# Reordering the steps in which an image leaves: stores between the scans, decays before squares, power between multiplications, adding DMAs thinned out, z fetched earlier

## The chip, the cores and the metric

The kernel runs on one core of a Trainium2 chip. The metric is the device time of one launch in microseconds (us). The five engines are called by their names and, in profile lines, by short forms: TensorE (PE for matmuls, PEld for weight loads), VectorE (DVE), ScalarE (ACT), GpSimd (POOL) and SyncE (SP), which here only issues DMAs. L891 in a profile line is line 891 of the kernel.

## The reference

The input is eight images of 128 x 128 positions with 128 channels. A first layer (an attention with a linear cost, a layer norm and a residual) gives x. A second layer, a selective scan in four directions, uses it. Cut to what matters, with `z` and `u` made from x by a projection and a small convolution, over L = 16384 positions and 256 channels:

```python
delta = softplus(dt_weight @ dt + dt_bias)          # per direction
dA    = exp(delta * A)
xc    = dA * xc + delta * u * B                     # a scan along L
y_dir = xc * C + u * D
...
y   = y0 + y1 + y2 + y3                             # the four directions, turned back
yz  = y * silu(z)
yn  = (yz - mean(yz)) / sqrt(var(yz) + 1e-5) * gamma + beta      # over the 256 channels
out = yn @ Wout
```

## The kernel before, in words

There are three stages: `layer0`, `layer1_front` and `layer1_scan`. The first two keep in DRAM what the third needs: `ubs` (u times B), `xps` (the rows for delta and for C, as three bfloat16 parts), `zs` (silu of z) and `gs` (the sums of u times D). The change touches the third stage alone, `layer1_scan`, which in the trace begins at about 5010 us of 10095.

The third stage walks 512 units. An output image has four slots, one for each direction, and a slot has NCH = 16 chunks of CH = 1024 positions: 8 x 4 x 16 units. All 256 channels lie as two halves c of 128 partitions. The sum y of one image stays in SBUF whole (`y`, 128 x 2 x 16384 float32). The first slot of an image (`place` 0) writes y, the other three add to it.

For every unit n, `step(n)` issues the following, and `in_order` makes each engine keep exactly the order in which its instructions are issued. So the text of `step` is the schedule: an engine never passes an instruction that waits.

- `load_rows` and `load` bring the rows (three buffers) and the unit `ubt` (1 MB, four buffers, three units ahead) through SyncE's queue. At the start of a slot, `load_rows` also loads small weights (L813, L814).
- `delta(n + 1, c)` multiplies the rows into PSUM (L873). `soften` is a softplus on ScalarE (L877), `decay` an exponential in place in PSUM (L881). The two functions need different tables, so each pair has a table load ahead of it.
- `weigh` multiplies the unit by the softened delta on GpSimd (L884).
- `scan` runs the recurrence on VectorE (L891 forwards, L893 backwards), once for each half c; `state` (L901) keeps the last column.
- `spread` makes C on all partitions with a matmul (L907). `emit` multiplies by C one step later on VectorE (L919 in the first slot; L924, L931 and L935 in the others), `gather` (L943, VectorE) and `add` (L950, GpSimd) add to y.

When the four slots of an image are through, its y leaves in 16 pieces of 1024 positions, one in each of the first 16 steps of the next image's first slot. `leaving` maps a step to the image and piece; `now`, `last` and `soon` are the pieces of this step, the step before and the next one. I call these steps the leaving steps. For a piece:

- `fetch` loads z (two tiles of 512 KB, a ring of five), `gate` multiplies y by z, the first half on GpSimd and the second on VectorE (L970), one step ahead.
- `square` (L973, ScalarE) writes the squares, `moments` (L983, TensorE) sums both over the channels, `keep` (L989, ScalarE) and `to_tokens` (L995, TensorE) turn the sums, `variance` (L999 to L1003, VectorE) makes the variance, and `deviation` (L1006, GpSimd) raises it to the power -0.5.
- `project` (L1013, TensorE) multiplies by Wout into the PSUM bank that the scan of the second half has just left. `store` (L1019, VectorE, and the DMA L1023) scales and writes out, one step later.

Two resources tie these together. PSUM has three pairs of banks, each of 1024 columns, (`px`) which delta, decay, scan, project and store pass on to each other in a ring. And the moments, the turned moments and the second spread share one bank (tag "pt"), so the second spread waits until `variance` has copied the moments (L999).

`add_d` (L844) is a DMA from GpSimd's queue which adds 1 MB of `gs` to a piece of y in SBUF. `summed` gives the step in which each piece has it.

Of the kernel before, what the change touches and what calls it, by code (L numbers as in the profile page):

```python
# [21 lines left out]
NC2 = 2  # L22
R = 8
K = 4
# [7 lines left out]
NCH = L // CH  # L32
# [655 lines left out]
def layer1_scan(ctx: ExitStack, tc, ubs, xps, zs, gs, dtw, dtb, a_log, gamma, beta, w_out, out):  # L688
# [15 lines left out]
    nc = tc.nc  # L704
# [128 lines left out]
    units = []  # L833
# [5 lines left out]
    ubt, sp, da, st = {}, {}, {}, {}  # L839
# [6 lines left out]
    def load_rows(n):  # L846
        sl, i = units[n]
        m = sl.at(i)
        if i == 0:
            sl.weights()  # L850
        rw = rws[n % 3]
        md = NCH - 1 - m if sl.dt_turned_back else m
        src = xps[sl.dt_image, sl.dt_order].rearrange("j r l -> (j r) l")
        for j in range(3):
            nc.sync.dma_start(rw[3 * NR * j : 3 * NR * j + 3 * NR, :], src[:, md * CH : md * CH + CH])
        nc.sync.dma_start(rw[96:99, :], xps[sl.b, sl.order, :, R + 1, m * CH : m * CH + CH])

    def load(n):
        sl, i = units[n]
        m = sl.at(i)  # L860
        ubt[n] = wp.tile([P, NC2, CH], F32, name="ubt", tag="ub", bufs=4)
        nc.sync.dma_start(ubt[n], ubs[sl.b, sl.order].rearrange("c p l -> p c l")[:, :, m * CH : m * CH + CH])

    def delta(n, c):
        sl, i = units[n]
        rw = rws[n % 3]
        da[n, c] = p = px.tile([P, CH], F32, name="px")
        for hf in range(2):
            if sl.dt_turned_back:
                src = rw[:, (1 - hf) * 512 : (1 - hf) * 512 + 512][:, ::-1]  # L870
            else:
                src = rw[:, hf * 512 : hf * 512 + 512]
            nc.tensor.matmul(p[:, hf * 512 : hf * 512 + 512], sl.dw[:, c * P : c * P + P], src, start=True, stop=True)  # L873

    def soften(n, c):
        sp[n, c] = t = wp.tile([P, CH], F32, name="sp", tag="sp", bufs=3)
        nc.scalar.activation(t, da[n, c], AF.Softplus)  # L877

    def decay(n, c):
        sl, i = units[n]  # L880
        nc.scalar.activation(da[n, c], sp[n, c], AF.Exp, scale=sa[:, sl.s, c : c + 1])  # L881

    def weigh(n, c):
        nc.gpsimd.tensor_tensor(ubt[n][:, c, :], ubt[n][:, c, :], sp.pop((n, c)), ALU.mult)  # L884

    def scan(n, c):
        sl, i = units[n]
        x, e = da[n, c], ubt[n][:, c, :]
        start = 0.0 if i == 0 else st[n - 1][:, c : c + 1]
        if sl.back:  # L890
            nc.vector.tensor_tensor_scan(e[:, ::-1], x[:, ::-1], e[:, ::-1], start, ALU.mult, ALU.add)  # L891
        else:
            nc.vector.tensor_tensor_scan(e, x, e, start, ALU.mult, ALU.add)  # L893
# [11 lines left out]
    def spread(n, hf, tag):  # L905
        cps[n, hf] = p = pe.tile([P, 1, GN], F32, name="pc", tag=tag)
        nc.tensor.matmul(p[:, 0, :], csel, rws[n % 3][:, hf * 512 : hf * 512 + 512], start=True, stop=True)  # L907

    def emit(n, hf):

        sl, i = units[n]
        h = ubt[n][:, :, hf * 512 : hf * 512 + 512]
        c = cps.pop((n, hf)).to_broadcast([P, NC2, GN])
        if sl.place == 0:
            v = sl.y_at(i, hf)
            split = "p c (a b) -> p c a b"
            nc.vector.tensor_tensor(v, h.rearrange(split, b=H), c.rearrange(split, b=H), ALU.mult)  # L919
            if hf == 1:  # L920
                ubt.pop(n)
            return
        if hf == 1:
            nc.vector.tensor_tensor(h, h, c, ALU.mult)  # L924
            return
        p = da.pop((n, 1))
        if sl.y_turned:
            ts[n] = p.rearrange("p (c b a) -> p c b a", c=NC2, a=GW)
            t = p.rearrange("p (c b a) -> p c a b", c=NC2, a=GW)
            split = "p c (a b) -> p c a b"  # L930
            nc.vector.tensor_tensor(t, h.rearrange(split, b=H), c.rearrange(split, b=H), ALU.mult)  # L931
        else:
            t = p.rearrange("p (c q) -> p c q", c=NC2)
            ts[n] = t.rearrange("p c (a b) -> p c a b", b=H)
            nc.vector.tensor_tensor(t, h, c, ALU.mult)  # L935
# [19 lines left out]
    def piece(m, hf):  # L955
        return y[:, :, (2 * m + hf) * GN : (2 * m + hf + 1) * GN]

    def mirrored(o, m, hf):
        p = 2 * m + hf
        return 2 * NCH - 1 - p if o % 2 == 1 else p  # L960

    def fetch(o, m):
        for hf in range(2):
            zt[m, hf] = z = wp.tile([P, NC2, GN], F32, name="z", bufs=5)
            p = mirrored(o, m, hf)
            nc.sync.dma_start(z, zs[o].rearrange("c p l -> p c l")[:, :, p * GN : p * GN + GN])

    def gate(o, m, hf, eng):
        z, ym = zt[m, hf], piece(m, hf)
        eng.tensor_tensor(z, ym[:, :, ::-1] if o % 2 == 1 else ym, z, ALU.mult)  # L970

    def square(m, hf):
        nc.scalar.activation(piece(m, hf), zt[m, hf], AF.Square)  # L973

    def moments(m):

        pm = pe.tile([P, GN], F32, name="pm", tag="pt")
        for c in range(NC2):
            for j in range(2):
                for hf in range(2):  # L980
                    at = 32 * (2 * j + hf)
                    v = piece(m, hf) if j else zt[m, hf]
                    nc.tensor.matmul(pm[at : at + 32, :], mean, v[:, c, :], start=(c == 0), stop=(c == NC2 - 1))  # L983
        pts[m, "rows"] = pm

    def keep(m):
        pm = pts[m, "rows"]
        pts[m, "rows"] = sr = wp.tile([P, GN], F32, name="sr", bufs=1)
        nc.scalar.copy(sr, pm)  # L989

    def to_tokens(m):
        sr = pts.pop((m, "rows"))
        pts[m] = p = pe.tile([P, GW, NC2, 2], F32, name="pq", tag="pt")
        for w in range(GW):
            nc.tensor.matmul(p[:, w], sr[:, w * H : w * H + H], sel, start=True, stop=True)  # L995
# [9 lines left out]
    def deviation(m):  # L1005
        nc.gpsimd.tensor_tensor(rst[m], rst[m], half, ALU.pow)  # L1006
# [17 lines left out]

    leaving, summed = {}, {}
    for o in range(B):
        for j in range(NCH):
            m = NCH - 1 - j if o % 2 == 1 else j  # L1030
            leaving[(o + 1) * K * NCH + j] = o, m
            summed[((o + 1) * K - 1) * NCH + j + 3] = o, m
    N = len(units)

    def step(n):
        live = 0 <= n < N
        then = n + 1 < N
        before = 1 <= n <= N
        now, last, soon, fresh = (leaving.get(n + i) for i in (0, -1, 1, 2))
        if before:  # L1040
            emit(n - 1, 0)
            if units[n - 1][0].place:
                gather(n - 1)
            emit(n - 1, 1)
        if n + 2 < N:
            load_rows(n + 2)
        if now:
            for hf in range(2):
                square(now[1], hf)
            moments(now[1])  # L1050
        if last:
            for hf in range(2):
                store(*last, hf)
        if live:
            for c in range(NC2):
                decay(n, c)
            for c in range(NC2):
                weigh(n, c)
        if soon:
            gate(*soon, 0, nc.gpsimd)  # L1060
        if then:
            delta(n + 1, 0)
        if now:
            keep(now[1])
            to_tokens(now[1])
        if live:
            scan(n, 0)
            da.pop((n, 0))
        if then:
            delta(n + 1, 1)  # L1070
        if live:
            scan(n, 1)
            state(n)
        if now:
            variance(now[1])
        if then:
            for c in range(NC2):
                soften(n + 1, c)
        if soon:
            gate(*soon, 1, nc.vector)  # L1080
        if live:
            spread(n, 0, "pc")
            spread(n, 1, "pt")
        if now:
            p = da.pop((n, 1)) if live else px.tile([P, CH], F32, name="px")
            for hf in range(2):
                project(now[1], hf, p[:, hf * 512 : hf * 512 + 512])
        elif live and units[n][0].place == 0:
            da.pop((n, 1))
        if before and units[n - 1][0].place:  # L1090
            add(n - 1)
        if now:
            deviation(now[1])
        if n in summed:
            add_d(*summed[n])
        if n + 3 < N:
            load(n + 3)
        if fresh:
            fetch(*fresh)

    with in_order(tc):
        for n in range(2):
# [73 lines left out]
```

## Time and profile before

| | us |
|---|---|
| median of three runs | 10100.93 |
| lowest and highest | 10088.13, 10116.6 |
| span of the profiled run | 10095.5 |

| engine | busy us | share of the span |
|---|---|---|
| VectorE | 8259.1 | 82% |
| GpSimd | 7140.6 | 71% |
| ScalarE | 7135.9 | 71% |
| TensorE, matmuls | 6506.4 | 64% |
| TensorE, weight loads | 3272.1 | 32% |

The shares are means over three stages with different limits, so they don't say what limits the third. The costs of one instruction that matter here, as the groups of the page and the trace give them:

| line | engine, operation | mean ns |
|---|---|---|
| L884 | GpSimd, weigh | 2482 |
| L970 | GpSimd, gate | 2387 |
| L1006 | GpSimd, power | 2349 |
| L950 | GpSimd, add (half a piece) | 1616 |
| L891, L893 | VectorE, scan | 2334 |
| L970 | VectorE, gate | 1523 |
| L1019 | VectorE, store (eight in a step) | 342 |
| L877, L881 | ScalarE, soften, decay | 1024, 1109 |
| L973 | ScalarE, square | 1054 |

A mean can hide two kinds of the same instruction. The gate on VectorE has a median of 1226 ns and a longest of 6372 ns; the power on GpSimd takes 1.66 us in one step of the trace and 2.48 in another.

### The profile page before, as it was taken

How to read it: one execution, taken by the hardware profiler on the slowest of the kernel's cores; microseconds unless marked ns; L12 is line 12 of the kernel's file. 1: busy time of each engine (PE TensorE's matmuls, PEld its weight loads, DVE VectorE, ACT ScalarE, POOL GpSimd, SP SyncE). 2: the span in 40 equal slices, each digit the busy share in tenths (PEclk: the TensorE clock that was granted, in tenths of full speed). 3: DMA queues.
4: the chain of work that ended last, by engine and by line, in shares of the span. 5: the costliest groups of instructions: out<-in, count | busy, mean ns of one | idle time of the engine just before them, and what ended most of it. 6: DMA issues, size and time to landing. Idle time of an engine off the chain costs nothing.

```text
span 10095.5 us, 89685 instructions
## 1 busy us (share of the span) xinstructions
PE 6506.4 (64%) x24190; PEld 3272.1 (32%) x24352; DVE 8259.1 (82%) x9060; ACT 7135.9 (71%) x8098; POOL 7140.6 (71%) x4224
## 2 busy tenths in 40 slices
PE   8889999988678667876433635436354363553735
PEld 5555555553223222322100403204032040320503
DVE  6556776566889888988799898998989989899797
ACT  5556655556788777777687686776867768677685
POOL 3444555455475667876589798897978979789697
PEclk9999999999889888988755756557565575655757
DMA  2333223324674778877657658576485764857748
GB/s 89 128 127 127 84 97 116 128 101 158 215 269 167 244 244 256 244 238 245 238 158 201 203 154 243 161 200 205 150 243 162 202 204 153 236 165 196 209 150 224
DMA packets 1034805, 1851.19 MB, mean 183 GB/s; under 512 B 274852, under 2 KB 500772, under 8 KB 1026112
## 3 DMA queue, kind: packets, MB, share of 16 engines
q1 hardware_dynamic: 999488, 1711.23, 52.0%
q0 software_dynamic: 34816, 134.23, 6.7%
q8 instruction: 199, 3.26, 0.1%
q14 instruction: 302, 2.47, 0.1%
HBM read 1153.03 MB, written 692.12 MB: 183 GB/s over the span
## 4 chain that ended last, share of the span: by engine, by line
DVE 30%; POOL 10%; issue 4%; DMA 4%; PE 1%; ACT 1%; SPq 0%; POOLq 0%; DVEq 0%; another core or an unknown queue 0%; ACTq 0%
DVE ubt L891 9%; DVE ubt L893 8%; POOL ubt L884 5%; DVE y L943 3%; DVE ubt L924 3%; DVE px L931 3%; POOL rstd L1006 2%; DVE r L1019 2%; POOL y L950 2%; DMA z<-zs 2%; DMA rows<-xps 1%; DMA ubt<-ubs 1%; POOL y L844 1%; POOL z L970 1%; DVE state L901 1%
## 5 line engine op out<-in xcount | busy, mean ns | idle before, releaser
L884 POOL TENSOR_TENSOR ubt<-ubt,sp 128x1024 f32<-128x1024 f32 x1024 | 2455.0, 2482 | 107.4 <-ACT sp L877 91.4
L873 PE MATMUL px<-rows,dtw 128*128 128x512 bf16 x1886 | 913.4, 578 | 2274.0 <-DVE y L943 882.6
L504 POOL TENSOR_TENSOR tap<-tap 128x1024 f32<-128x1024 f32 x512 | 1206.7, 2367 | 717.4 <-ACT tap L502 618.0
L512 DVE SCALAR_TENSOR_TENSOR acc<-xb,cw,acc 128x1024 f32<-128x1024 f32 x1024 | 1320.5, 1290 | 51.0
L494 PE MATMUL acc<-xi,wt 128*128 128x512 f32 x2048 | 982.9, 624 | 569.9 <-ACT ures L519 569.5
L877 ACT ACTIVATE sp<-px 128x1024 f32<-128x1024 f32 x1024 | 1041.2, 1024 | 398.1 <-PE px L873 307.9
L950 POOL TENSOR_TENSOR y<-y,ubt 128x512 f32<-128x512 f32 x768 | 1187.9, 1616 | 117.3 <-DVE ubt L924 113.0
L873 PEld LDWEIGHTS <-dtw 128*128 128x128 bf16 x2048 | 180.2, 115 | 3061.7 <-issue 906.5
L891 DVE TENSOR_TENSOR_SCAN ubt<-px,state,ubt 128x1024 f32<-128x1024 f32 x480 | 1100.6, 2334 | 10.9 <-POOL ubt L884 7.6
L881 ACT ACTIVATE px<-sp,sa 128x1024 f32<-128x1024 f32 x1024 | 1103.2, 1109 | 6.1
L893 DVE TENSOR_TENSOR_SCAN ubt<-px,state,ubt 128x1024 f32<-128x1024 f32 x480 | 1100.5, 2334 | 8.0 <-POOL ubt L884 4.3
L502 ACT ACTIVATE tap<-xb,cw 128x1024 f32<-128x1024 f32 x768 | 833.4, 1139 | 154.2 <-DVE acc L510 91.2
L877 ACT ACT_TABLE_LOAD x512 | 656.9, 1283 | 314.9 <-PE px L873 288.8
L1013 PEld LDWEIGHTS px<-wg,z 128*128 128x128 f32 x4096 | 722.9, 274 | 212.8 <-issue 203.3
L494 PEld LDWEIGHTS acc<-xi,wt 128*128 128x128 f32 x2048 | 395.9, 199 | 1138.0 <-ACT ures L519 675.1
L274 POOL TENSOR_TENSOR q<-q,qs 128x512 f32<-128x512 f32 x256 | 271.4, 1060 | 680.8 <-DVE qs L273 680.8
L1013 PE MATMUL px<-wg,z 128*128 128x128 f32 x4096 | 715.8, 356 | 0.0
L881 ACT ACT_TABLE_LOAD x512 | 656.9, 1283 | 9.1
L907 PE MATMUL pc<-rows,csel 128*128 128x512 bf16 x1024 | 532.1, 601 | 179.7 <-DVE mv L999 170.2
L1006 POOL TENSOR_TENSOR rstd<-rstd,half 128x8 f32<-128x8 f32 x128 | 300.7, 2349 | 422.9 <-DVE rstd L1003 420.7
L467 PE MATMUL pxb<-xi,wi 128*128 128x512 f32 x1024 | 498.5, 609 | 29.0 <-ACT xh L607 24.7
L1019 DVE SCALAR_TENSOR_TENSOR r<-px,rstd,bw 128x128 f32<-128x128 f32 x1024 | 276.5, 342 | 293.4 <-issue 229.6
(159 smaller groups left out, 15373.1 us busy)
## 6 DMA issues: line engine op xcount, KB each, us to landing
ubt<-ubs SPq DMA_DIRECT2D x512, 1024.0 KB
zs<-z SPq DMA_DIRECT2D x512, 256.0 KB
ubs<-ures SPq DMA_DIRECT2D x256, 512.0 KB
ubs<-turned SPq DMA_DIRECT2D x256, 512.0 KB
y<-gs POOLq DMA_DIRECT2D x128, 1024.0 KB, 13.1
z<-zs SPq DMA_DIRECT2D x256, 512.0 KB
rows<-xps SPq DMA_DIRECT2D x1536, 60.0 KB
xi<-x SPq DMA_DIRECT2D x120, 576.0 KB
```

Source lines behind the costliest of these rows:

```text
L494: nc.tensor.matmul(acc[:, s, :], wt[:, j, c, :], x, start=(j == 0), stop=(j == len(ON_PE) - 1))
L502: nc.scalar.activation(t, at(n, c, *d), AF.Copy, scale=cw[:, c, tap(*d) : tap(*d) + 1])
L504: nc.gpsimd.tensor_tensor(sums[n, c], sums[n, c], t, ALU.add)
L512: nc.vector.scalar_tensor_tensor(acc, at(n, c, *d), cw[:, c, tap(*d) : tap(*d) + 1], acc, ALU.mult, ALU.add)
L873: nc.tensor.matmul(p[:, hf * 512 : hf * 512 + 512], sl.dw[:, c * P : c * P + P], src, start=True, stop=True)
L877: nc.scalar.activation(t, da[n, c], AF.Softplus)
L881: nc.scalar.activation(da[n, c], sp[n, c], AF.Exp, scale=sa[:, sl.s, c : c + 1])
L884: nc.gpsimd.tensor_tensor(ubt[n][:, c, :], ubt[n][:, c, :], sp.pop((n, c)), ALU.mult)
L891: nc.vector.tensor_tensor_scan(e[:, ::-1], x[:, ::-1], e[:, ::-1], start, ALU.mult, ALU.add)
L893: nc.vector.tensor_tensor_scan(e, x, e, start, ALU.mult, ALU.add)
L950: nc.gpsimd.tensor_tensor(v[:, c], v[:, c], h[:, c], ALU.add)
L1013: nc.tensor.matmul(po[:, w, :], z[:, c, w * H : w * H + H], wg[:, c, :], start=(c == 0), stop=(c == NC2 - 1))
```

## The change

The order within `step` is written anew, and the dictionaries that place the DMAs are changed:

- Stores of the last piece stand between the two scans, where they stood ahead of both.
- Decays (and the first weigh) stand ahead of the squares and moments.
- The power of the last piece stands in the next step between the two weighs, where it stood at the end of its own step.
- Both halves of delta stand after the stores, and `to_tokens` after them and after the softens; before, `to_tokens` stood between the two halves.
- Both gates stand after the spreads; the one on GpSimd stood after the weighs, with nothing of GpSimd in between, so its place in GpSimd's own order is the same but for the power.
- The adding DMAs come every 1.5 steps instead of every step: piece j in step 3 + (3j + 1) // 2 of the image's last slot, so that seven of the sixteen fall into leaving steps.
- z for the first two pieces is fetched four steps ahead of leaving, where it was two; for the others it stays two.
- In the first slot of an image the unit load is issued early in the step.

What it is for: to let the stores wait less for the projection, to have the first scan fed earlier, to take load off the DMA while an image finishes, and to have z in SBUF when the first pieces leave.

The core of the diff:

```diff
-    leaving, summed = {}, {}
+    leaving, summed, fetched = {}, {}, {}
     for o in range(B):
+        n = (o + 1) * K * NCH
         for j in range(NCH):
-            m = NCH - 1 - j if o % 2 == 1 else j
-            leaving[(o + 1) * K * NCH + j] = o, m
-            summed[((o + 1) * K - 1) * NCH + j + 3] = o, m
+            e = o, NCH - 1 - j if o % 2 == 1 else j
+            leaving[n + j] = e
+            fetched[n + j - 2 if j > 1 else n + j - 4] = e
+            summed[n - NCH + 3 + (3 * j + 1) // 2] = e
...
         if n + 2 < N:
             load_rows(n + 2)
+        if first and n + 3 < N:
+            load(n + 3)
+        if live:
+            for c in range(NC2):
+                decay(n, c)
+            weigh(n, 0)
+        if last:
+            deviation(last[1])
+        if live:
+            weigh(n, 1)
         if now:
             for hf in range(2):
                 square(now[1], hf)
             moments(now[1])
+        if live:
+            scan(n, 0)
+            da.pop((n, 0))
         if last:
             for hf in range(2):
                 store(*last, hf)
-        if live:
+        if then:
             for c in range(NC2):
-                decay(n, c)
-            for c in range(NC2):
-                weigh(n, c)
-        if soon:
-            gate(*soon, 0, nc.gpsimd)
-        if then:
-            delta(n + 1, 0)
+                delta(n + 1, c)
         if now:
             keep(now[1])
+        if then:
+            for c in range(NC2):
+                soften(n + 1, c)
+        if now:
             to_tokens(now[1])
-        if live:
-            scan(n, 0)
-            da.pop((n, 0))
-        if then:
-            delta(n + 1, 1)
         if live:
             scan(n, 1)
             state(n)
         if now:
             variance(now[1])
-        if then:
-            for c in range(NC2):
-                soften(n + 1, c)
-        if soon:
-            gate(*soon, 1, nc.vector)
         if live:
             spread(n, 0, "pc")
             spread(n, 1, "pt")
+        if soon:
+            gate(*soon, 0, nc.gpsimd)
+            gate(*soon, 1, nc.vector)
...
-        if now:
-            deviation(now[1])
+        if n + 3 < N and not first:
+            load(n + 3)
         if n in summed:
             add_d(*summed[n])
-        if n + 3 < N:
-            load(n + 3)
-        if fresh:
-            fetch(*fresh)
+        if n in fetched:
+            fetch(*fetched[n])
```

More of the change, by code (lines that the diff above doesn't have):

```diff
@@ L1038, in step @@
         before = 1 <= n <= N
-        now, last, soon, fresh = (leaving.get(n + i) for i in (0, -1, 1, 2))
+        now, last, soon = (leaving.get(n + i) for i in (0, -1, 1))
+        first = before and units[n - 1][0].place == 0
         if before:
             emit(n - 1, 0)
-            if units[n - 1][0].place:
+            if not first:
                 gather(n - 1)
@@ L1089, in step @@
             da.pop((n, 1))
-        if before and units[n - 1][0].place:
+        if before and not first:
             add(n - 1)
-        if now:
-            deviation(now[1])
+        if n + 3 < N and not first:
+            load(n + 3)
         if n in summed:
             add_d(*summed[n])
-        if n + 3 < N:
-            load(n + 3)
-        if fresh:
-            fetch(*fresh)
+        if n in fetched:
+            fetch(*fetched[n])
     with in_order(tc):
```

## The prediction

> **What bounds the kernel now.** I first read the page's busy times and slices for the stage that the change touches, then the windows of single steps in that stage, then its waits, then the timeline of one step.
>
> ```profile
> PE 6506.4 (64%) x24190; PEld 3272.1 (32%) x24352; DVE 8259.1 (82%) x9060; ACT 7135.9 (71%) x8098; POOL 7140.6 (71%) x4224
> DVE  6556776566889888988799898998989989899797
> ```
>
> No engine is full over the span, and the last half of the slices (the scan stage, from about 5010 us) has VectorE at 8 to 9 tenths with dips. The dips come once per image. A window from first scan to first scan of neighbouring steps gives the length of a step:
>
> ```profile
> 8047.20:8066.87 19.67, 4.99 (x18) 1.74 (x22) 9.74 (x8) 9.47 (x9) 10.41 (x7) 0.50 0.68 188
> 8066.87:8086.56 19.69, 11.42 (x70) 6.19 (x64) 11.53 (x19) 9.53 (x10) 13.28 (x8) 0.76 0.74 206
> 8086.56:8105.06 18.50, 11.08 (x57) 8.45 (x60) 14.89 (x19) 9.00 (x9) 12.15 (x6) 0.68 1.05 288
> 8179.00:8192.60 13.60, 10.51 (x63) 8.19 (x64) 10.82 (x19) 9.38 (x10) 9.48 (x5) 0.75 0.67 209
> 8292.82:8424.13 131.31, 46.89 (x96) 9.24 (x97) 130.14 (x97) 108.32 (x96) 122.01 (x62) 0.50 0.50 154
> 7990.40:7998.60 8.20, 2.96 (x7) 0.57 (x6) 8.13 (x7) 6.77 (x6) 8.20 (x6) 0.50 1.05 275
> ```
>
> (Columns: length, busy PE, PEld, DVE, ACT, POOL, clock, DMA share, GB/s.) Sixteen plain steps take 131.31, 8.2 each, and VectorE fills 130.14 of it: nothing to gain there. The sixteen steps in which an image leaves take 13.6 once settled with VectorE busy only 10.82, and 18.5 to 19.7 at the start, with VectorE half idle. The stretch from the last step ahead of leaving to the end of leaving (17 steps, by the first scans in VectorE's timeline) is 246.7, 245.6, 247.7, 246.7, 245.6, 249.4 and 247.2 us for the seven images that leave while the next scans: mean 247.0. The eighth leaves alone, in the last 143.5 us.
>
> What makes 13.6 of 10.82 is in the waits of a settled stretch and in the timeline:
>
> ```profile
> DVE r L1019 <- issue: 24.2, 9, 2.7
> PE pc L907 <- DVE mv L999: 13.7, 8, 1.7
> 8175.48 6.12 PE L1013 MATMUL px<-wg,z 128*128 128x128 f32 x32
> 8181.70 2.16 DVE L1019 SCALAR_TENSOR_TENSOR r<-px,rstd,bw 128x128 f32<-128x128 f32 x8 [2.65 <-issue]
> 8183.77 4.58 DVE L891 TENSOR_TENSOR_SCAN ubt<-px,state,ubt 128x1024 f32<-128x1024 f32 x2
> 8188.47 0.17 DVE L999 COPY mv<-pq 128x16 f32<-128x16 f32 x1
> 8189.06 6.16 PE L1013 MATMUL px<-wg,z 128*128 128x128 f32 x32
> ```
>
> The project ends at 8175.48 + 6.12 = 8181.60 and the stores begin at 8181.70, so "issue" hides the wait for it (in the tail the waits name it: PE px L1013). The loop is project 6.16, stores 2.1, scans 4.6, then the copy of the moments that frees the bank in front of the second spread, and project again: 13.6. The start of leaving is another matter:
>
> ```profile
> 8034.58 12.77 SPq L813 DMA_DIRECT2D dtw<-wparts  x9
> 8051.40 0.89 SPq L966 DMA_DIRECT2D z<-zs  x2
> 8057.53 2.34 POOL L970 TENSOR_TENSOR z<-y,z 128x1024 f32<-128x1024 f32 x1 [9.26 <-DMA z<-zs]
> 8059.29 1.66 DVE L970 TENSOR_TENSOR z<-y,z 128x1024 f32<-128x1024 f32 x1 [7.51 <-DMA z<-zs]
> ```
>
> The adding DMA of every step fills the DMA (share 1.05 at 275 GB/s in the window at 7990), small weight loads take 12.77 us to issue, z is asked for only behind them and arrives 6 to 8 us later.
>
> **What the Trainium skill says.** "SBUF — State Buffer", section "SBUF: two separate sides": VectorE with two SBUF inputs and a GpSimd operation that reads SBUF exclude each other for a whole instruction. The trace agrees:
>
> ```profile
> 8094.61 5.10 POOL L884 TENSOR_TENSOR ubt<-ubt,sp 128x1024 f32<-128x1024 f32 x2
> 8095.56 5.24 DVE L970 TENSOR_TENSOR z<-y,z 128x1024 f32<-128x1024 f32 x1 [3.47 <-DMA z<-zs]
> 9982.61 2.35 POOL L970 TENSOR_TENSOR z<-y,z 128x1024 f32<-128x1024 f32 x1 [3.49 <-DMA z<-zs]
> 9982.70 2.30 DVE L1003 TENSOR_SCALAR rstd<-rstd 128x8 f32<-128x8 f32 x1
> ```
>
> A 1.22 us gate took 5.24 beside two weighs, and a 0.17 us operation 2.30 beside a GpSimd gate; the scans and stores, with one operand in PSUM, do not show it. "TensorE: Matmul & The Clock Gate", section "What's actually happening": the clock is half unless TensorE was busy of late. Here the project takes 6.16 at a mean clock of 0.75 and 3.82 in the tail at 0.94.
>
> **The change part by part.** I lay out one settled leaving step from the start of emit (0), with the measured durations.
>
> Stores between the scans: emit ends at 2.3, scan 0 at 4.6, stores at 6.75, scan 1 at 9.0, copy of moments 9.1 to 9.25, three variance operations to 9.85, the VectorE gate to 10.95. The project of this step starts at about 9.7 and ends 3.82 to 6.16 later, at 13.5 to 15.9, which is 2.6 to 5.0 of the next step; its stores are due at 4.6. The wait of 2.65 is gone or nearly so. VectorE alone then gives 10.95.
>
> New waits of that order: delta of the next unit needs the PSUM bank that the stores read, so it starts at 6.8 and, now both halves together, holds back to_tokens on TensorE: delta 1.2 to 2.0, to_tokens 1.0 to 1.8, so the moments come at 9.0 to 10.6 where VectorE wants them at 9.1. The loop through TensorE is stores 2.2 + delta + to_tokens + copy 0.3 + spread 0.4 to 0.6 + project = 9.0 with all fast, 11.3 with only the project slow, 13.1 with all slow.
>
> Decays ahead of squares: ScalarE has softens to about 9.6, table 1.28 and decays 2.15 to 13.0, squares 2.1, then moments on TensorE (1.2 to 2.4 after the last square), keep 0.6, table 1.28: ready for the softens again at about 7.4 of the step, before delta is there (7.5). So ScalarE hides behind delta, and decay is never waited for by scan 0. I cost this at nothing.
>
> Power between the weighs: GpSimd has weigh 2.35, power 1.66, weigh 2.35, gate 2.36 = 8.7, with an adding DMA (1.2) 9.9, under 10.95. Queued behind the power is weigh 1, awaited by scan 1 at 6.75; it ends at about 4. Hidden. But the first weigh of the next unit is released by its soften at about 8.6 and runs to 10.95. It reads SBUF while VectorE comes to its variance operations at 9.3. By the lock they wait until 10.95, end at 11.5, and the gate at 12.7: +1.6. Power itself needs the variance, so GpSimd then stands and VectorE gets through. If the weigh starts after 9.8 the gate goes first, and the step is 11.0. I take 12.6, since soften follows the stores by fixed times.
>
> Adding DMAs every 1.5 steps: one costs (1.05 - 0.50) x 8.2 = 4.5 us of DMA time. In the last slot the load falls from 8.6 to 4.1 + 3.0 = 7.1 per 8.2 us; the small delays there (3, 0, 2, 2, 0, 3, 2 us beyond 15 x 8.2) should half vanish: -6 in all. Seven of the sixteen now fall into leaving: 0.67 x 13.6 = 9.1, + 3.0 = 12.1 of DMA time at a reachable share of 1.05 = 11.6 us a step, still below 12.6.
>
> z sooner: the first two pairs are asked for two steps earlier, four of five buffers. Each pair (1 MB) takes about 3.4 us of DMA, worked out from a plain step: 0.50 x 8.2 = 4.1 us for the unit's 1 MB and 0.19 MB of rows, which briefly overfills two steps and leaves 3 us of backlog that the unit loads, two steps ahead, absorb. Step by step: the last step before leaving becomes emit 3.66 + scans 4.6 + state + gate 1.2 and a lock wait, 11.5; the first leaving step about 12 (no stores yet, but GpSimd still has the two adds, 3.5). The extra load order for the first slot only moves a load ahead of the stores in SyncE's queue: nothing.
>
> Sum: 11.5 + 12 + 15 x 12.6 = 212.5 against 247.0, -34.5, times 7 = -241.5; -6 from the slot before. The tail's 7.35 us loop runs through TensorE and has no scans: 0; adds during it may cost some us, earlier z gives as much back. 10101 - 247.5, about 9853.
>
> **The rivals.**
> - No lock wait: the weigh starts late or the variance slips through. For it: in the settled stretch of before they never meet. Against: the release times above. 15 x 11.1: 190 per image, -57 x 7 - 6: 9696.
> - A TensorE loop or late z takes the wait's place: half clock in most of the chain, 13.1, or z behind adding DMAs, 13.5. For it: clock 0.75 now, and the second z half still waits for a project. Against: denser work raises the clock. 15 x 13.3: 223, -24 x 7 - 6: 9927.
> - Slower: the gate is held back not by one weigh but by power and the second weigh as well, as at 8095.56 (+4.0). 10.95 + 1.6 + 4.0 = 16.5 a step: 271, +24 x 7: 10269. Against: such back-to-back running followed an adding DMA there, and power needs VectorE first.
>
> **How the numbers follow.** Chances: forecast 50, no lock wait 18, TensorE or z 20, slower 12 in 100. The range 9695 to 9970 holds the first three but for the edges. Faster 0.86 (the first three, less a remainder), same 0.03, slower 0.11.
>
> **What would show it.** Right: "DVE r L1019 <- issue" gone, settled steps near 12.6 with variance or gate operations of 1.5 to 2.5 us beside L884, no idle of 7 us for z at the start. Wrong: settled steps of 11.0 (lock), of 13 or more with VectorE waiting for the moments (TensorE) or z, or gates of 4 to 6 us in most steps.

## The result, and the profile after

| | before | changed |
|---|---|---|
| median, us | 10098.44 (10088.13 to 10116.6) | 9866.85 (9859.01 to 9874.97) |
| ratio, 95% interval | | 0.9769 [0.9752, 0.9786] |
| span of the profiled run, us | 10095.5 | 9860.3 |

The change made the kernel 2.3% faster, 232 us by the medians; 9853 was predicted. I read the same views in the same order. First the page's busy times and VectorE's slices:

```profile
PE 6392.8 (65%) x24352; PEld 3116.9 (32%) x24352; DVE 8364.1 (85%) x9060; ACT 7121.7 (72%) x8098; POOL 7143.2 (72%) x4224
DVE  6556775566898888888889999999999999999996
```

The dips in the last half of the slices, one for each image, are gone. But VectorE is busy for 8364.1 us where it was 8259.1, with as many instructions (9060): some of its instructions have become longer. The windows of steps (length, busy PE, PEld, DVE, ACT, POOL, clock, DMA share, GB/s), for the image that was shown of before. The first two are the last two steps ahead of leaving, the next two are single leaving steps, each from first scan to first scan; the last holds some five leaving steps:

```profile
7891.96:7903.30 11.34, 2.72 (x6) 0.72 (x6) 8.33 (x8) 5.71 (x6) 6.96 (x5) 0.50 1.06 301
7903.30:7917.58 14.28, 3.47 (x8) 0.94 (x10) 9.49 (x7) 6.66 (x7) 11.52 (x7) 0.50 0.62 163
7929.67:7940.89 11.22, 9.71 (x64) 5.76 (x62) 10.80 (x19) 9.17 (x10) 10.27 (x6) 1.00 1.02 298
7952.13:7967.16 15.03, 9.68 (x62) 5.59 (x58) 14.89 (x18) 12.03 (x12) 11.52 (x6) 0.98 1.02 313
8050.00:8113.24 63.24, 47.42 (x328) 36.43 (x328) 62.46 (x97) 49.49 (x48) 48.76 (x22) 0.92 0.76 227
```

In the leaving steps VectorE is now full (14.89 of 15.03, 62.46 of 63.24), yet the step of 15.03 holds 4.09 us more of VectorE than that of 11.22, with one instruction fewer. In these lines TensorE's clock is 0.92 to 1.00 where it was 0.75. Ahead of leaving (the first two lines) VectorE still idles by 3.0 and 4.8 us. The DMA is full in the first of these steps (1.06), but not in the second (0.62).

VectorE's waits over the whole last stage (what waited and for what: us in total, times, longest), before:

```profile
DVE r L1019 <- issue: 229.6, 83, 4.0
DVE z L970 <- DMA z<-zs: 118.1, 22, 8.9
...
DVE px L935 <- PE pc L907: 3.5, 4, 1.2
```

and after:

```profile
DVE mv L999 <- PE pq L995: 47.8, 19, 6.5
DVE px L935 <- PE pc L907: 31.8, 15, 3.9
DVE r L1019 <- DMA out<-r: 20.1, 10, 4.3
...
DVE z L970 <- DMA z<-zs: 7.1, 3, 3.4
...
DVE r L1019 <- issue: 0.4, 1, 0.4
```

The stores' wait for the project (229.6) is gone from the leaving steps, and the gate's wait for z (118.1) is down to 7.1, in the tail. L935 has grown, one emit that waits for a spread in the last steps ahead of leaving. L999, VectorE's copy of the moments, has grown from 26.0 (before, all of it in the tail) to 47.8: 25.4 in the first leaving steps of the seven images, 22.4 in the tail. What fills VectorE in their place is in no list of waits, as it lies inside the instructions. VectorE's timeline in one settled step (start, us, instruction):

```profile
7973.91 0.17 DVE L999 COPY mv<-pq 128x16 f32<-128x16 f32 x1
7974.11 2.02 DVE L1001 TENSOR_TENSOR rstd<-mv 128x8 f32<-128x8 f32 x1
7976.17 0.17 DVE L1002 TENSOR_TENSOR rstd<-mv,rstd 128x8 f32<-128x8 f32 x1
7976.37 0.17 DVE L1003 TENSOR_SCALAR rstd<-rstd 128x8 f32<-128x8 f32 x1
7976.45 1.23 DVE L970 TENSOR_TENSOR z<-y,z 128x1024 f32<-128x1024 f32 x1
...
7987.02 2.34 DVE L1002 TENSOR_TENSOR rstd<-mv,rstd 128x8 f32<-128x8 f32 x1
```

and GpSimd's at the same time:

```profile
7973.77 2.34 POOL L884 TENSOR_TENSOR ubt<-ubt,sp 128x1024 f32<-128x1024 f32 x1 [1.48 <-issue]
7976.62 2.58 POOL L1006 TENSOR_TENSOR rstd<-rstd,half 128x8 f32<-128x8 f32 x1 [0.51 <-DVE rstd L1003]
...
7986.99 2.34 POOL L884 TENSOR_TENSOR ubt<-ubt,sp 128x1024 f32<-128x1024 f32 x1 [0.77 <-issue]
```

The weigh begins at 7973.77 and ends at 7976.11; an operation of 128 x 8 on VectorE which takes 0.17 us elsewhere ends just behind it, at 7976.13. In the next step the same happens to L1002 (7986.99 to 7989.33, and 7989.36). GpSimd's next instruction, the power, needs VectorE's L1003, so nothing of GpSimd runs when the gate (1.23) begins, and the gate is not held. In the step of 15.03 two operations are held: L1002 for 2.25 us beside GpSimd's gate, which z had made late, and L1003 for 2.27 us beside the weigh behind it. L1003 has one input tensor only, so the hold isn't confined to operations with two inputs in SBUF, as the prediction's words have it; its own L1003 line (2.30) shows this too.

To see where the time went I added up the last stage by slots, from first scan to first scan in VectorE's timeline, over all images. Slot 0 is the one in which the image before leaves, slot 3 the one that gets the adding DMAs, the tail is from the last scan to the end:

| us | slot 0 | slot 1 | slot 2 | slot 3 | tail | sum |
|---|---|---|---|---|---|---|
| before | 1705 | 1050 | 1051 | 1134 | 143.5 | 5084 |
| changed | 1497 | 1065 | 1051 | 1099 | 154.8 | 4867 |
| changed, a second time | 1501 | 1065 | 1051 | 1100 | 155.6 | 4873 |

(Some 14 us between slots 0 and 1 are no cost: with the stores behind the first scan, that scan, which is the mark, comes 2 us earlier in a leaving step, and there are seven such boundaries.) The sum falls by 217 and 211. The rest of the difference of the two profiled spans, 18 us, lies ahead of the stage: the first scan is at 4993 in this profile and at 5012 before. Whether it belongs to the change is asked below.

### The profile page after: what moved, and what is told of

Same layout as the page of the kernel before. It is cut to its first block, busy times and chain, and to the rows that moved or that the text cites. A ratio compares the mean times of both kernels' runs of the same rounds, so it can differ in the third digit from the quotient of the medians.

```text
span 9860.3 us, 90189 instructions
## 1 busy us (share of the span) xinstructions
PE 6392.8 (65%) x24352; PEld 3116.9 (32%) x24352; DVE 8364.1 (85%) x9060; ACT 7121.7 (72%) x8098; POOL 7143.2 (72%) x4224
## 5 line engine op out<-in xcount | busy, mean ns | idle before, releaser
L884 POOL TENSOR_TENSOR ubt<-ubt,sp 128x1024 f32<-128x1024 f32 x1024 | 2442.4, 2431 | 250.2 <-ACT sp L877 154.5
L873 PE MATMUL px<-rows,dtw 128*128 128x512 bf16 x2048 | 947.0, 564 | 2249.0 <-DVE y L943 1012.3
L950 POOL TENSOR_TENSOR y<-y,ubt 128x512 f32<-128x512 f32 x768 | 1154.2, 1537 | 149.1 <-DVE ubt L924 145.9
L881 ACT ACTIVATE px<-sp,sa 128x1024 f32<-128x1024 f32 x1024 | 1103.1, 1109 | 6.1
L1013 PEld LDWEIGHTS px<-wg,z 128*128 128x128 f32 x4096 | 563.5, 221 | 118.8 <-issue 113.4
L1013 PE MATMUL px<-wg,z 128*128 128x128 f32 x4096 | 563.3, 304 | 0.0
L943 DVE TENSOR_TENSOR y<-y,px 128x1024 f32<-128x1024 f32 x384 | 468.6, 1220 | 14.2
L924 DVE TENSOR_TENSOR ubt<-ubt,pc 128x1024 f32<-128x1024 f32 x384 | 466.2, 1214 | 0.0
```

The lines of the kernel that those rows point to most:

```text
L943: nc.vector.tensor_tensor(v, v, ts.pop(n), ALU.add)
L950: nc.gpsimd.tensor_tensor(v[:, c], v[:, c], h[:, c], ALU.add)
L1013: nc.tensor.matmul(po[:, w, :], z[:, c, w * H : w * H + H], wg[:, c, :], start=(c == 0), stop=(c == NC2 - 1))
```

## The experiments

My theory was that of the prediction: the stores' wait goes, the lock between the next unit's weigh and the variance operations takes a part of it back, and z in time mends the start. The rivals were a TensorE loop or DMA that sets the step, and GpSimd's order as the limit. Each kernel below was timed in three rounds beside the kernel before; `after_again`, `wav_again`, `both` and `both_last` in five, side by side on one chip. "Slot 0" and so on are the sums of the table above.

**The parts alone.** `order_only` has the new order of the step and the old times of the DMAs:

```diff
-            fetched[n + j - 2 if j > 1 else n + j - 4] = e
-            summed[n - NCH + 3 + (3 * j + 1) // 2] = e
+            fetched[n + j - 2] = e
+            summed[n - NCH + 3 + j] = e
```

> The new order of step with the old DMA times (an adding DMA in every step, all z two steps ahead). My account: the two halves of the change act apart. The order takes the 2.65 us wait of the stores out of the settled steps and puts a lock wait of 0.7 to 3 us into most of them (12.3 against 13.6, some 13 steps, seven images: -120), while the first leaving steps stay near 19 us because z is late: about 9980 us. Rival, the DMA times do it all: within 0.5% of before, 10050 to 10100. Rival, the order does it all: 9870.

Measured: 9944.82, 0.9851 [0.9837, 0.9866], 149 us less than before. Slot 0 is 1538. Settled steps take mostly 11.4 to 12.9, as in the changed kernel, but the first two leaving steps still some 18 each: z is late whatever the order.

`dma_only` has the new times of the DMAs and the old order:

```diff
-            summed[((o + 1) * K - 1) * NCH + j + 3] = o, m
...
+            fetched[n + j - 2 if j > 1 else n + j - 4] = e
+            summed[n - NCH + 3 + (3 * j + 1) // 2] = e
...
-        if fresh:
-            fetch(*fresh)
+        if n in fetched:
+            fetch(*fetched[n])
```

> The old order of step with the new DMA times (adding DMAs every 1.5 steps, the first two z pairs four steps ahead). My account: the first three long steps of each image shrink from 57.5 us to about 40, the settled steps stay at 13.6 with the stores waiting for the project: -17 x 7 = -120, about 9980. Rival, the DMA times do it all: 9870. Rival, the order does it all: 10080 to 10100.

Measured: 9991.57, 0.99 [0.9885, 0.9915], 102 us less. Slot 0 is 1626: the leaving steps begin at 10.9 to 12.6 and settle at 13.6 again. The two halves of the change are thus 149 and 102 us, which add up to a little more than the 232 of both. They act in different steps.

`fetch_only` has the old order and the old adding DMAs, and only z sooner:

```diff
-            summed[((o + 1) * K - 1) * NCH + j + 3] = o, m
...
+            fetched[n + j - 2 if j > 1 else n + j - 4] = e
+            summed[n - NCH + 3 + j] = e
...
-        if fresh:
-            fetch(*fresh)
+        if n in fetched:
+            fetch(*fetched[n])
```

> The old order, adding DMAs in every step, only the first two z pairs four steps ahead. If the late z alone made the long first steps: as dma_only, about 9980. If the full DMA queue made them, so that thinning the adding DMAs is what counts: above 10050, with z still awaited for several us.

Measured: 10041.45, 0.9953 [0.9938, 0.9967], 53 us less. Slot 0 falls to 1622, as far as with all DMA times new, but slot 3 rises from 1134 to 1164. The two last steps ahead of leaving took 8.2 and 18.8 to 21.3 in the kernel before; here they take 15.7 to 17.4 and 15.0 to 16.3. VectorE's waits of this kernel say for what:

```profile
DVE r L1019 <- issue: 249.1, 92, 4.0
DVE px L935 <- PE pc L907: 78.6, 15, 8.1
```

The emit waits up to 8.1 us for the spread, and TensorE for the rows that come ahead of it: 424 us in the whole stage, where it was 326 before and is 161 in `dma_only`. z comes in time and the rows don't: early z needs room in the DMA, which the thinned adding DMAs give. That is the part that I had as two separate terms.

**Parts undone.** `sums_every_step` is the changed kernel with an adding DMA in every step:

```diff
-            summed[n - NCH + 3 + (3 * j + 1) // 2] = e
+            summed[n - NCH + 3 + j] = e
```

> The changed kernel with the adding DMAs in every step again (the early z kept). If thinning them matters: the last slot before leaving fills the DMA, rows come late, the first leaving steps wait; 20 us or more slower than the changed kernel, 9885 to 9930. If it does not, or if adding DMAs in leaving steps cost as much as they save: 9860 to 9875 or faster.

Measured: 9914.42, 0.9812 [0.9796, 0.9828], 48 us slower than the changed kernel. Slot 3 is 1158 for 1099 (its last two steps mostly take 14 to 16.5 each), slot 0 is 1487 for 1497, and the tail 141.0 for 154.8. Thinning out is worth 59 us ahead of leaving and costs 10 during it and 14 in the tail.

`stores_first` is the changed kernel with the stores ahead of both scans:

```diff
+        if last:
+            for hf in range(2):
+                store(*last, hf)
         if live:
             scan(n, 0)
             da.pop((n, 0))
-        if last:
-            for hf in range(2):
-                store(*last, hf)
```

> The changed kernel with one thing undone: the stores of the last piece stand ahead of both scans again. If the place of the stores carries the gain of the settled steps: the stores wait for the project again, steps of 12.5 to 13.6, 9880 to 9990 (middle 9930). Rival: with stores 2.3 us earlier, delta, softens and the first weigh come earlier too, the weigh no longer meets the variance operations, and steps fall to 11.0 to 11.5: 9730 to 9790.

Measured: 9976.1, 0.988 [0.9864, 0.9897], 109 us slower than the changed kernel and 15 faster than `dma_only`, which is within the intervals of the two. Most steps settle at 13.6 again. Its waits:

```profile
DVE r L1019 <- issue: 80.0, 43, 3.6
DVE r L1019 <- POOL ubt L884: 69.8, 32, 2.6
...
DVE r L1019 <- PE px L1013: 46.6, 21, 2.7
```

All three lines are waits for the project, 196 us in all: in each of these waits the stores begin within 0.15 us of the project's end, also where the profile names the weigh (L884), which had ended earlier, and the power earlier still. Waits for the power (L1006) are 16.0 us.

`power_late` is the changed kernel with the power at the end of its own step:

```diff
-        if last:
-            deviation(last[1])
         if live:
             weigh(n, 1)
...
+        if now:
+            deviation(now[1])
```

> The changed kernel with the power at the end of its own step again, ahead of both weighs of the next. The first weigh then stands behind the power, which needs the variance, so it can't hold the variance operations back; but the weigh comes 1.66 us or more later and the first scan waits for it. By the lock account: variance operations all 0.17 us, first scan waiting about 1.5 us, step about 12.6, so 9850 to 9890. Rival, the place of the power is what made the settled steps shorter: 13.6, 9970.

Measured: 9979.79, 0.988 [0.9863, 0.9898], 113 us slower than the changed kernel. The higher of the two expected times came; the lock's account alone was some 100 us too low. VectorE's timeline of one step:

```profile
8005.43 0.17 DVE L1001 TENSOR_TENSOR rstd<-mv 128x8 f32<-128x8 f32 x1
8005.63 0.17 DVE L1002 TENSOR_TENSOR rstd<-mv,rstd 128x8 f32<-128x8 f32 x1
8005.83 0.17 DVE L1003 TENSOR_SCALAR rstd<-rstd 128x8 f32<-128x8 f32 x1
8005.91 1.23 DVE L970 TENSOR_TENSOR z<-y,z 128x1024 f32<-128x1024 f32 x1
...
8012.26 2.35 DVE L891 TENSOR_TENSOR_SCAN ubt<-px,state,ubt 128x1024 f32<-128x1024 f32 x1 [2.87 <-POOL ubt L884]
```

and GpSimd's:

```profile
8006.08 2.55 POOL L1006 TENSOR_TENSOR rstd<-rstd,half 128x8 f32<-128x8 f32 x1 [3.01 <-DVE rstd L1003]
8008.58 1.23 POOL L844 DMA_DIRECT2D y<-gs  x1
8009.39 5.13 POOL L884 TENSOR_TENSOR ubt<-ubt,sp 128x1024 f32<-128x1024 f32 x2
```

No variance operation is held. But GpSimd stands for 3.01 us until the variance is there, then has the power and, in this step, an adding DMA in front of its weighs, and the first scan waits 2.87 us for the first of them. Over the whole stage the scans wait 243 us for weighs, against 5.0 in the changed kernel. A chain through GpSimd has taken the place of the one through TensorE. So the two moves help only together: with the new DMA times the old order gives 9992, the new order without the one or the other move gives 9976 and 9980, and with both 9867.

**The lock.** `weigh_after_variance` moves the last of the three variance operations to GpSimd, ahead of the first weigh. The weigh can then not begin before the other two are through:

```diff
-        nc.vector.tensor_scalar(rstd, rstd, 0.0, EPS1, ALU.max, ALU.add)
+
+    def shift(m):
+        nc.gpsimd.tensor_scalar(rst[m], rst[m], 0.0, EPS1, ALU.max, ALU.add)
...
+        if last:
+            shift(last[1])
+        if live:
             weigh(n, 0)
```

> The changed kernel with the last operation of the variance (clamp and eps, 128 x 8) moved from VectorE to GpSimd, where it stands ahead of the first weigh of the next step. It costs GpSimd 0.2 us and makes that weigh wait until VectorE has done the variance. By the lock account the variance operations are 0.17 us again and the step falls from a mean of 12.4 to 11.2 (VectorE alone 10.8): -1.2 x 14 x 7, about 9750. Rival, the waits would only move (the gate behind the weigh, the scan behind the weigh, or TensorE's loop): 9830 to 9870.

Measured: 9812.38, 0.9715 [0.97, 0.9729]. It went as the lock has it in kind, and fell short of my size. A second time (the two operations on GpSimd are the clamp and the power, which was there already), as `wav_again`, on the same chip as the changed kernel (`after_again`):

> The lock theory's kernel once more: two of the variance's five small operations on GpSimd, ahead of the next unit's first weigh. 9805 to 9820, as the first time (9812), some 54 us below the changed kernel on the same chip. If the first difference came of the chip, it is less than 20 us.

Measured: 9807.71, 0.9719 [0.9706, 0.9732], against 9869.69, 0.9783 [0.9768, 0.9798]: 62 us less, and slot 0 is 1435 for 1501. Two settled steps of it in VectorE's timeline:

```profile
7990.94 0.17 DVE L1001 TENSOR_TENSOR rstd<-mv 128x8 f32<-128x8 f32 x1
7991.14 0.17 DVE L1002 TENSOR_TENSOR rstd<-mv,rstd 128x8 f32<-128x8 f32 x1
7991.29 1.23 DVE L970 TENSOR_TENSOR z<-y,z 128x1024 f32<-128x1024 f32 x1
...
8000.76 1.13 DVE L1021 SCALAR_TENSOR_TENSOR r<-px,rstd,bw 128x128 f32<-128x128 f32 x4 [2.33 <-DMA out<-r]
...
8004.45 2.35 DVE L1001 TENSOR_TENSOR rstd<-mv 128x8 f32<-128x8 f32 x1
```

and in GpSimd's:

```profile
8004.41 2.36 POOL L970 TENSOR_TENSOR z<-y,z 128x1024 f32<-128x1024 f32 x1 [5.46 <-DMA z<-zs]
```

In the first step nothing is held. In the second the stores wait 2.33 us for a buffer whose write to DRAM is not through, and GpSimd's own gate, 5.46 us late for want of z, holds the variance. Both are the DMA. Over the 15 leaving steps behind the first, the time that the variance operations take beyond 0.17 each is 21.3 us an image in the changed kernel and 2.2 here, 19 less; VectorE's idle time rose from 3.6 to 13.2, and its gate, held for 0.0 before, is held for 1.9. Some 9 of the 19 us come back as time: (1501 - 1435) / 7. The idle time is mostly waits of the stores for a buffer (5.1 us an image), of the scans for the weighs (3.4) and of the gate for z (1.6). Where nothing else waits, a step is 10.9 to 11.1, VectorE's own work.

The weighs are late in part because the clamp ahead of them takes longer than the 0.2 us that I had expected. Two clamps of GpSimd:

```profile
7437.06 0.25 POOL L1005 TENSOR_SCALAR rstd<-rstd 128x8 f32<-128x8 f32 x1 [1.19 <-DVE rstd L1002]
7991.41 1.22 POOL L1005 TENSOR_SCALAR rstd<-rstd 128x8 f32<-128x8 f32 x1
```

At the first, VectorE's gate had not begun, as it waited for z. At the second it had run since 7991.29, and the clamp ends 0.11 us behind it. Of the 128 clamps 15 take 0.25 to 0.3 us and 103 take 1.1 to 1.25: the lock has in part changed sides.

One rival is the issue of an adding DMA (L844) on GpSimd. In the changed kernel 12 of the 112 variance operations that took over 0.3 us began while one ran, and ten of these began before the weigh did by the profile, up to 3.57 us long. But the issue stands where it stood in `wav_again`, from 7990.19 to 7991.42 in the first step above, and the two variance operations under it take 0.17 us each. So the issue by itself does not hold them; why these ten wait from before the weigh's start stays open.

**The small loads.** `weights_early` loads the small weights of a slot 14 units sooner, in place of just when the image's last steps run:

```diff
-        if i == 0:
+        if n == 0:
             sl.weights()
+        if i == 2 and n + NCH < len(units):
+            units[n + NCH][0].weights()
```

> The changed kernel with the small weights of a slot loaded 14 units earlier, while no adding DMA runs. If the 11.4 us that their issue takes on SyncE makes the rows late and so the 2, 3.5 and 2.8 us of waiting on VectorE in the last two steps before leaving and in the first: these waits go, -8 x 7 = -55, about 9810. Rival, the rows are late because the DMA is full, whatever is issued ahead of them: 9850 to 9870.

Measured: 9866.61, 0.9766 [0.975, 0.9782], no change. In its trace, however, the last step ahead of leaving takes 10.6 to 11.1 where the changed kernel has 10.7 to 14.3, and slot 3 is 1081 for 1099; slot 0 and the tail give back 7 of these 18. With an interval of 16 us to either side, the time of this run can't show so little. So it was tried again on top of the other, as `both`:

> That and the slot's small weights loaded 14 units earlier. By the full DMA (rows and z late because adding DMAs, units, rows and z together fill it, not because of what is queued ahead of them): no more than the first alone, 9800 to 9820. By the queue (rows late behind 11 us of small loads, which now matters since the lock hides it no longer): the two last steps ahead of leaving fall from 14 and 11 to 11 each, 3 us x 7, so about 9790.

Measured: 9794.29, 0.9701 [0.9688, 0.9715], 13 us less than `wav_again` on the same chip; slot 3 is 1079 for 1096. The intervals overlap, so that some 15 us lie in this queue is likely and not settled. What the queue looks like in the changed kernel, in SyncE's timeline (the time is that of issuing):

```profile
7890.58 3.46 SPq L966 DMA_DIRECT2D z<-zs  x2
7895.33 11.39 SPq L813 DMA_DIRECT2D dtw<-wparts  x9
...
7907.43 1.21 SPq L855 DMA_DIRECT2D rows<-xps  x3
```

The nine small loads hold the queue for 11.39 us, and the rows of the next unit are asked for only behind them. Without them a part stays: in `weights_early` TensorE still waits up to 8.3 us for rows in these steps, three of whose loads take 7.67 us to issue.

**The tail, and the 18 us ahead of the stage.** `after_again` is the changed kernel, unaltered:

> The changed kernel once more, beside the others on one chip. In its first profile the first stage (before the first L512 instruction) ended some 18 us earlier than in every other profile, with nothing changed there. If that is chance of one execution, the first scan of the last stage is at about 5007 to 5016 us here instead of 4993, and the time is 9860 to 9875 all the same. If it belongs to the change (the way the program is laid out), it is at 4993 again.

Measured: 9869.69, 222 us below the kernel before beside it, and the first scan is at 5016 us. In the other profiles, of before and of all kernels here, it is between 5007 and 5016. So the 18 us in the first stages of the first profile belong to that execution or its chip and not to the change.

`both_last` is `both`, with the adding DMAs of the last image in every step:

```diff
-            summed[n - NCH + 3 + (3 * j + 1) // 2] = e
+            summed[n - NCH + 3 + ((3 * j + 1) // 2 if o < B - 1 else j)] = e
```

> The same, and for the last image alone the adding DMAs in every step, as before the change. The tail, from the last scan to the end, took 154.8 with thinned adding DMAs and 141.0 with one in every step (143.5 in the kernel before), as nothing of another image follows there for the DMA to make room for. So 11 to 14 us less than the run without: about 9795 if that is 9808. If the tail's length comes of the new order of the work, no difference.

Measured: 9779.64, 0.9692 [0.9679, 0.9706], 14.7 us less than `both`. The intervals overlap, but the tail is 141.1 for 157.4 in the traces, and it was 141.0 for 154.8 in the same comparison above. The same 30 us of the tail in the windows, `both`:

```profile
9700.00:9730.00 30.00, 23.75 (x164) 15.38 (x164) 14.41 (x40) 7.31 (x8) 17.07 (x11) 0.89 0.91 237
```

and `both_last`:

```profile
9700.00:9730.00 30.00, 26.95 (x231) 20.45 (x231) 15.43 (x49) 11.45 (x13) 20.97 (x13) 1.00 0.76 216
```

With less of the DMA taken (0.76 for 0.91), TensorE gets through 231 matmuls in place of 164. This is the fastest of all kernels here, 312 us below the kernel before.

## Why the prediction was right, and where it was not

- **The stores' wait: right.** "DVE r L1019 <- issue" went from 229.6 us to 0.4. `stores_first` brings 196 us of waits of the stores for the project back and loses 109 us.
- **The lock on the variance: right in kind, and in size as a mean.** I had 1.6 us in each of 15 steps; measured 21.3 us an image, 1.4 a step, but unevenly: from 0 to 4.7 us, with some hold in 93 of 105 steps. Steps behind the first leaving one: 184.6 us for 15, plus 2 for the moved mark, is 12.44 each, where I had 12.6. The Trainium skill ("SBUF — State Buffer", section "SBUF: two separate sides") says that whichever of the two operations starts first gets the ports for the whole instruction and the other blocks; the pair 7973.77 and 7974.11 above shows it. That the hold was caused by the weigh is shown by `weigh_after_variance`; that removing it brings all of it back is not so, because waits for the DMA and for the weighs stand next.
- **The TensorE loop does not bind: right for the settled steps.** Over the fifteen leaving steps behind the first, the mean clock is 0.90 where it was 0.75, and single steps have 0.73 to 1.00. The project's mean over the leaving steps went from 5.8 us to 4.5; it takes under 4 us in 63 of 112, where it did in 7. VectorE waits for the moments in the first leaving step, and else only in the tail.
- **The slower rival, a gate held by power and second weigh, did not come.** In those fifteen steps the gate was held for 0.0 us.
- **Decays and ScalarE at nothing: right.** Scans wait for L881 for 1.8 us in all of the last stage. The early unit load was also put at nothing. Neither it nor the move of the decays was tried by itself.
- **Power between the weighs "hidden": right, and the reason it matters was missed.** I gave the move no worth. `power_late` shows that without it the first scan waits for GpSimd and 113 us are lost.
- **The last step ahead of leaving and the first leaving step: too short.** I had 11.5 and 12, measured 13.2 and 13.1 (19.6 and 19.7 before). For the last step, what failed is "leaves 3 us of backlog that the unit loads, two steps ahead, absorb". The rows don't absorb it: they stand behind small loads, which are issued in a full DMA (1.06) and take 11.39 us. In `weights_early` the same step takes 10.6 to 11.1. For the first leaving step a term was missing: VectorE waits 2.8 to 4.3 us there for the moments, and no run moved this.
- **The slot before: wrong sign.** I had -6 in all. The first 15 steps of slot 3 went from a mean of 124.7 us to 125.8, +8 over seven images. The small delays inside the slot did vanish (those steps are 8.2 each now), but the last of the 15 takes 9.8 to 11.7 where it took 8.2. That is the early z, whose price falls into the steps where it is fetched and not where it is used: `fetch_only`, which moves z alone, lengthens this step to 15.7 and more. `fetch_only` and `sums_every_step` show that thinning out the adding DMAs pays for it, with 59 us instead of 6.
- **The tail: wrong.** I had 0, with "adds during it may cost some us, earlier z gives as much back"; measured +11. Seven adding DMAs now fall into it where there were three, and `both_last` gets 14.7 us by going back to three.

The last three points cost 2.8 x 7 = 20, 14 and 11 us that I did not have, 45 in all; settled steps 0.16 us shorter than I had them gave back 15 x 7 x 0.16 = 17. The 28 left are nearly what the table of the slots shows: 217 us gained where I had 247. The profiled difference of 235 comes nearer to the forecast only because of the 18 us ahead of the stage, which are luck and not the change; the timed differences, 232 and 222 the second time, have the spread of the runs in them.

## What to carry to other kernels

When a wait is removed from a loop with several engines, write down the next chain through each engine: here the chain through TensorE gave steps of 13.6 and the one through GpSimd mostly 12.5 to 14.1, and the new order without the one or the other move was worth 12 to 15 us, within the intervals of the runs, of the 125 that both brought. Look at busy time that grows with the same number of instructions: a lock lies inside the instructions and in no list of waits. An earlier prefetch isn't free when the DMA is full; price it in the steps where it is issued, with what is queued behind it, and undo what was spread out to make room where nothing follows, as in the tail.

## What the runs showed of the hardware that I had not expected

- The lock holds the smallest operations as it holds large ones, and both ways: in the lines above 0.17 us became 2.02 to 2.35 beside a weigh or a GpSimd gate, and GpSimd's power 1.66 became 2.58 when VectorE's gate had begun 0.17 us ahead of it. In the kernel before, 105 of the 128 powers are held so already.
- GpSimd's clamp of 128 x 8 takes 0.25 us where VectorE's takes 0.17, and mostly 1.15 to 1.22 because VectorE's gate holds it. On GpSimd it was still worth the move, since it made the weigh wait.
- The granted clock of TensorE rose as VectorE stopped waiting: in the leaving steps it was 0.90 in the mean where it had been 0.75, and the median project took 3.73 us where it had taken 6.19, without a change to it.
- Two executions of one program, on one chip or on two, differed by 23 us in the first two stages, which take 5000 (4993 and 5016 at their end), more than several of the effects above. A single profile can't show effects of that size unless it is read stage by stage.
